# A two-layer cross-attention kernel: shared image values in layer 1, contexts laid out in pairs, and a fixed order for the first loads

## The chip, the cores and the metric

The kernel runs on one core of a Trainium2 chip. The metric is the device time of one execution in microseconds, lower is better. The engines are TensorE (PE, matrix products), VectorE (DVE), ScalarE (ACT), GpSimd (POOL) and SyncE (SP, which here issues nearly all DMAs).

## The reference

Two attention layers follow each other on x (16 images, 256 queries, 320 channels = 20 heads of 16). The context of an image has 256 tokens of 512 numbers. In layer 1, 77 are text tokens and 179 image tokens; in layer 2, 252 are text and 4 image. With s = 1/4:

```python
q = x @ Wq; k_text = text @ Wk; v_text = text @ Wv; ip_k = ip @ Wk_ip; ip_v = ip @ Wv_ip
text_out = softmax(q_h @ k_h.T * s) @ v_h                      # by head
scores = q_h @ ip_k_h.T * s
text_probs = softmax(q @ k_text.T * s)                         # all 320 channels, without heads
sem = (text_probs @ text) @ ip.T * s                           # 256 x 179
ip_out = (softmax(scores + 0.5 * sem) * spatial_mask) @ ip_v_h
x = (text_out + ip_out) @ Wout + bout + x
```

The second layer has the same form, with sem from the text probabilities of each head and normalized vectors.

## The kernel before

Each image of layer 1 is worked off in five slots of four heads; slot k = 5 b + g belongs to image b and heads 4g to 4g+3. Images 2c and 2c+1 form pair c. A matrix operand is split into a high and a low half (fp32r), and `prod` (L320) makes a product as three matmuls for each of the four 128-row tiles of the contexts: 12 matmuls.

In a slot PE computes S (L874: queries by keys, 128 queries in each of two halves), of which DVE takes the maxima of text and image columns. The maxima are transposed (L881), cast into `mt` and sent by DMA into a row of `qs`, the stack of queries; `ks` is the stack of keys, read from DRAM (`kd`), where the keys were stored with text first and image behind. Both stacks have 77 more rows for the semantic scores, which come from M (text tokens by image tokens, `tokens0`, the products of 77x192) and the text probabilities (`semantic0`, the matmuls X<-kb,q of L792). Then PE computes T, the scores with keys on partitions, less the maxima (L896); ACT exponentiates (L899) four pieces of 128x512, POOL multiplies each by `rs` (L902), and PE takes the products as moving operand with the values `vr` as weights (L934, `values0`, called from `attend0`), 24 matmuls a slot. The attend of slot k-1 stands in slot k.

The values of an image (`values0_`) are three products of 128 context tokens by 320 channels: tokens 0 to 127 by the text weights `wC`, tokens 0 to 127 by the image weights `wD`, tokens 128 to 255 by `wD`. Masks zero the rows that aren't text or image. In `values0` the value tile 0 is used by the first 16 of the 24 matmuls (text from tile 0, image from tile 0), and tile 1 by the last 8.

When each step of a task stands in the order is set by a table of slot times, STEPS: the name of a task (`k0` keys of a pair, `q0e`/`q0o` queries of the even and the odd image, `v0e`/`v0o` values, `m0e`/`m0o` tokens, `s0e`/`s0o` semantic, `c0` closing of an image; a 1 for layer 2, `w..` weights) and the slots, counted from the image's or pair's first, at which its steps are written. PE runs in exactly the order written; on the other engines a scheduler may reorder until `begun`. The steps ahead of the first slot are written one after the other in `begin`, and the first contexts and weights are loaded by `all_halves`, which issues the load of a tile and, when its ring is full, the casts of an older one. Loads of later contexts go through `context` and `in_turn`, with POOL making the low halves of a pair's second two tiles into `ctb` and its first two into `cta`.

## Time and profile before

| | |
|---|---|
| three runs | 1450.29, 1452.26, 1454.2 us |
| profiled execution | 1451.59 us, span 1449.8 us, granted clock 0.994 |
| PE, DVE, POOL, ACT busy | 97, 81, 79, 65% of the span |
| DMA | 215.74 MB, mean 149 GB/s |
| first T matmuls (L896) | 54.96 us |
| last value matmuls of layer 1's steady part, first of layer 2 | the stage 510.9 to 664.8 us |

A row of a timeline has the start in us from the span's begin, the duration of what was found in one piece, the engine, the line, the operation and the tiles (out<-in), the shapes and the count; in brackets the idle time ahead of it and what ended it. SPq rows are the times in which SP's queue issues DMAs; the data lands later. PEld is the load of PE's weights, which overlaps the products.

### The profile page before, as it was taken

What the parts mean: (1) busy time and instruction counts of PE and PEld (TensorE: products, weight loads), DVE (VectorE), ACT (ScalarE), POOL (GpSimd) and SP (SyncE); (2) the same over time, 40 slices, a digit from 0 to 9 for tenths busy, and PEclk for the clock granted to TensorE, in tenths of its full rate; (3) what the DMA queues carried; (4) which work ended last, traced back from release to release, by engine and by line L of the source; (5) the groups of instructions that cost most, each with busy time, mean ns of one, the idle gap of its engine ahead of it and who ended that gap; (6) DMA issues with size and microseconds to landing.
All of it is one profiled execution on the core that took longest, in us unless ns stands there. A gap on an engine that the chain in (4) does not pass through costs nothing.

```text
span 1449.8 us, 35042 instructions
## 1 busy us (share of the span) xinstructions
PE 1401.7 (97%) x12166; PEld 1157.8 (80%) x12166; DVE 1174.2 (81%) x2570; ACT 937.6 (65%) x2075; POOL 1152.3 (79%) x1181
## 2 busy tenths in 40 slices
PE   7899999999999999889999999999999999999998
PEld 6788888888888888577777788878878888888865
DVE  5477777777777788867888888988998889888887
ACT  5567676767676776755666666666666666566553
POOL 4269797979787878887778887788778877887785
PEclk9999999999999999999999999999999999999999
DMA  6866575665656578575544444544454445444411
GB/s 200 197 161 181 143 186 147 163 169 155 168 151 171 145 201 232 133 188 155 158 123 124 143 141 125 154 137 140 130 150 138 139 135 149 139 136 131 130 33 50
DMA packets 236284, 215.74 MB, mean 149 GB/s; under 512 B 57834, under 2 KB 222732, under 8 KB 236108
## 3 DMA queue, kind: packets, MB, share of 16 engines
q1 hardware_dynamic: 233886, 212.53, 53.4%
q8 instruction: 97, 1.59, 0.5%
q10 hardware_dynamic: 2222, 0.98, 0.3%
q14 instruction: 79, 0.65, 0.2%
HBM read 127.32 MB, written 85.16 MB: 147 GB/s over the span
## 4 chain that ended last, share of the span: by engine, by line
PE 52%; DVE 3%; POOL 1%; issue 1%; ACT 0%; DMA 0%; ACTq 0%; DVEq 0%; POOLq 0%
PE X L1075 18%; PE X L325 9%; PE X L725 6%; PE P L1088 5%; PE T L1018 4%; PE S L1023 3%; PE P L1090 2%; PE X L1209 1%; PE X L651 1%; PE P L1055 1%; DVE mn L1024 1%; PE P L934 1%; POOL P L902 0%; DVE wt L1078 0%; POOL wt L1066 0%
## 5 line engine op out<-in xcount | busy, mean ns | idle before, releaser
L902 POOL TENSOR_TENSOR P<-P,rs 128x512 f32<-128x512 f32 x320 | 412.4, 1313 | 136.1 <-ACT P L899 136.0
L1075 PE MATMUL X<-ctb,gm 128*128 128x512 f32 x1120 | 293.3, 403 | 0.7 <-DVE wt L1078 0.7
L1066 POOL TENSOR_TENSOR wt<-P,ctb 128x512 f32<-128x512 f32 x212 | 268.1, 1293 | 0.0
L899 ACT ACTIVATE P<-T 128x512 f32<-128x512 f32 x320 | 174.7, 594 | 101.8 <-PE T L896 83.7
L1024 DVE TENSOR_REDUCE mn<-S 128x4 fp32r<-128x1008 f32 x160 | 192.1, 1200 | 58.7 <-PE S L1023 56.8
L1075 PEld LDWEIGHTS X<-ctb,gm 128*128 128x128 f32 x1120 | 202.5, 190 | 38.5 <-DVE wt L1078 0.9
L1078 DVE TENSOR_TENSOR wt<-X,wt 128x512 f32<-128x512 f32 x240 | 159.7, 682 | 4.2 <-PE X L1075 3.9
L1030 ACT ACTIVATE P<-T 128x512 f32<-128x512 f32 x212 | 115.2, 598 | 58.3 <-PE T L1018 56.6
L1080 POOL TENSOR_TENSOR wt<-wt 128x512 f32<-128x512 f32 x80 | 103.5, 1294 | 60.2 <-DVE wt L1078 60.0
L876 DVE TENSOR_REDUCE mn<-S 128x4 fp32r<-128x716 f32 x160 | 142.5, 890 | 0.0
L1065 ACT ACTIVATE ctb<-P 128x512 fp32r<-128x512 f32 x212 | 122.4, 625 | 29.4 <-PE X L1075 20.6
L934 PE MATMUL P<-P,vr 128*32 128x256 f32 x1920 | 123.7, 388 | 0.0
L725 PE MATMUL X<-ho,wF 128*128 128x256 f32 x768 | 109.0, 286 | 2.2 <-DVE ho L974 1.2
L725 PEld LDWEIGHTS X<-ho,wF 128*128 128x128 f32 x768 | 100.5, 189 | 8.8 <-DVE ho L974 2.7
L725 PE MATMUL X<-hq,wE 128*128 128x256 f32 x720 | 102.7, 286 | 4.6 <-ACT hq L706 3.3
L725 PEld LDWEIGHTS X<-hq,wE 128*128 128x128 f32 x720 | 96.4, 193 | 8.3 <-ACT hq L706 3.8
L875 DVE TENSOR_REDUCE mn<-S 128x4 fp32r<-128x308 f32 x160 | 74.8, 468 | 23.2 <-PE S L874 22.9
L945 DVE STREAM_TRANSPOSE nt<-P 128x512 f32<-128x512 f32 x80 | 57.1, 714 | 39.2 <-PE P L934 38.9
L934 PEld LDWEIGHTS P<-P,vr 128*32 128x32 f32 x1920 | 56.1, 110 | 40.8 <-issue 4.9
L874 PE MATMUL S<-ks,qs 125*128 125x256 f32 x480 | 85.7, 301 | 2.2 <-DMA ks<-kd 1.7
L874 PEld LDWEIGHTS S<-ks,qs 125*128 125x128 f32 x480 | 64.4, 189 | 28.2 <-issue 24.1
L325 PE MATMUL X<-cta,wA 128*128 128x252 f32 (+3 forms) x534 | 78.8, 292 | 7.9 <-ACT wA L244 5.7
(231 smaller groups left out, 3275.3 us busy)
## 6 DMA issues: line engine op xcount, KB each, us to landing
qd<-q SPq DMA_DIRECT2D x80, 256.0 KB
qs<-qd SPq DMA_DIRECT2D x160, 112.0 KB
ks<-kd SPq DMA_DIRECT2D x160, 112.0 KB
rawc<-in_cT_dram SPq DMA_DIRECT2D x60, 256.0 KB
kd<-kst SPq DMA_DIRECT2D x50, 256.0 KB
qs<-qd SPq DMA_DIRECT2D x60, 192.0 KB
ks<-kd SPq DMA_DIRECT2D x60, 192.0 KB
qd<-q SPq DMA_DIRECT2D x64, 128.0 KB
```

What stands on the lines that cost most here:

```text
L325: last = mm(out, lhs(a, k), rhs(b, k), start=i == 0, stop=i == len(terms) - 1)
L725: mm(pp, w(s, k, slice(m * 128, (m + 1) * 128)), a[:, t], start=i == 0, stop=i == len(terms) - 1)
L874: mm(sp[:, h], Q[: XROW + T0, h, t * 128 : (t + 1) * 128], K[: XROW + T0, h], start=True, stop=True)
L876: anchor(nc.vector.tensor_reduce(mn[:, 1, :, t], sp[:, :, T0:], axis=AX.X, op=ALU.max))
L899: exp = anchor(nc.scalar.activation(pt, st[p], AF.Exp, scale=SCALE))
L902: anchor(nc.gpsimd.tensor_mul(pt, pt, rs[:, t : t + 1].to_broadcast([128, 2, S])))
L934: mm(pv[32 * s : 32 * s + 32, o : o + S], v[:, vt, h : h + 32], P[k, s // 2][:, t, s % 2], start=vt < 2, stop=vt != 1,)
L1024: anchor(nc.vector.tensor_reduce(maxes[k + 2][:, :, t], sp[:, :, :T1], axis=AX.X, op=ALU.max))
L1065: nc.scalar.activation(R[k, u][:, t], P[k, u][:, t], AF.Copy, scale=0.5)
L1066: anchor(nc.gpsimd.tensor_sub(W[k, u][:, t], P[k, u][:, t], f(R[k, u][:, t])))
L1075: mm(yp, gm[:, gb], R[k, u][:, kt], start=i == 0, stop=i == len(blocks[n]) - 1)
L1078: nc.vector.tensor_mul(product, yp, w[:, n])
```

## The change

- The contexts of a pair of layer 1 lie in one tile of 538 columns: 77 text of the even image, 179 image of the odd image, a gap of 26 zero columns, 179 image of the even image, 77 text of the odd. Each tile is loaded in three pieces (`bring`) instead of one.
- `values0_` makes two products for an even image and three for an odd one: the tile that holds image columns of both is multiplied once and evacuated twice, with masks, into the values of both images. For an even image the tile with the shared rows is 0; for an odd image it is 1, and `values0` uses it in the first 16 of the 24 matmuls. `attend0` sees to it that the shared product has been made.
- Text keys multiply 2 x 78 instead of 2 x 96 columns, the semantic scores of an image 154 instead of 192, tokens 180 instead of 192. The keys of an image lie in `kd` with text first for one of the pair and image first for the other, and the two indicator rows (which tell text from image columns) are in `kd` too: a load of the K stack brings 50 rows instead of 48.
- M is copied with all 256 columns into `ks`, before 179.
- In `project` the products with low halves of the right side come after those of the high ones.
- The first contexts and weights are loaded and cast in an order that is written out (BEGIN): of the contexts the text columns first, x of image 0 and the query weights next, image columns after them. Text keys are made tile by tile of the contexts.
- The output of the last image is sent in three pieces, each when it is done.
- Many entries of STEPS are other numbers.

```diff
+NI = S - T0
+GAP = 2 * T0 - 128
+PW = 2 * S + GAP
+TX, IM = (slice(NI, S), slice(0, T0)), (slice(0, NI), slice(T0, S))
+CT, CI = (PW - T0, 0), (T0, S + GAP)
+MIXED = (1, 0)
...
-    "k0": (-14.4, -13.3, -13, -12.4, -12, -10.8, -10.4, -9.8, -9.4, -8.8, -8.4,),
+    "k0": (-14.4, -13.3, -13, -12.4, -12, -10.8, -10, -9.4, -9, -8.4, -8,),
...
+BEGIN = """
+W2 C0 W0 C1 W1 C2 C3 W3 X0 Q0 Q1 Q2 c0 w0 T0 c1 w1 T1 c2 w2 T2 c3 w3 T3 I0 I1 q0:0 q0 q1 I2 I3 K0 K1 K2 q0:0
+i3 K3 e0 q2 V0 i0 i1 n0 q0:0 e1 e2 V1 V2 q0:0 i2 q0:0 q0:1 k0 k1 m0t:0 l1 q0:0 k2 l0 k3 l2 l3 V3 U0 U1 U2 U3
...
+    def bring(raw, src):
+
+        if src.shape[-1] == 2 * S:
+            for to, at, n in (0, 0, T0), (T0, S + T0, NI), (S + GAP, T0, S):
+                dma(raw[..., to : to + n], src[..., at : at + n])
+        else:
+            dma(raw, src)
...
     def values0_(b):
-        ct, i = ct0[b // 2], b % 2
-        V = vr[(b + 2) % 3]
-        for t, (w,), lo, sc in ((0, wv0, 0, tmask[:, 0:1]), (1, wvi0, 0, tmask[:, 1:2]), (2, wvi0, 128, 1.0)):
+        j, ring = 1 - b % 2, lambda b: vr[(b + 2) % 3]
+        V = ring(b)
+        parts = [(0, wv0, (PW - 128, 0)[j], 1), (2, wvi0, (CI[0], CI[1] + NI - 128)[j], 0)]
+        nc.vector.tensor_copy(vcols(V, V0W)[:, 0:2, :, 16], vmasks[j].unsqueeze(2).to_broadcast([128, 2, H]))
+        if b % 2:
+            parts.insert(0, (1, wvi0, S + T0 - 128, 1))
+        for t, (w,), lo, masked in parts:
             vp = bank()[:, :320]
-            prod(vp, lambda s, k: ct(s, k)[:, i, lo : lo + 128], lambda s, k: w(s, k), 4)
-            nc.scalar.activation(
-                vcols(V, V0W)[:, t, :, 0:16], vp.rearrange("p (h d) -> p h d", d=D), AF.Copy, scale=sc
-            )
+            prod(vp, lambda s, k: ct0[b // 2][k][:, s, lo : lo + 128], lambda s, k: w(s, k), 4)
+            for i in (j,) if t != 1 else (1, 0):
+                scale = vmasks[i][:, t : t + 1] if masked else 1.0
+                nc.scalar.activation(
+                    vcols(ring(b - i if t == 1 else b), V0W)[:, t, :, 0:16], vp.rearrange("p (h d) -> p h d", d=D), AF.Copy, scale=scale
+                )
+            if t == 1:
+                results["mixed", b // 2] = True
             yield
...
-        terms = [(s, k, t) for k in range(2) for s, t in ((0, k), (0, 3 + k), (1, k))] + [(0, 2, 2), (1, 2, 2)]
+        terms = [(s, k, k) for k in range(2) for s in range(2)] + [(0, 0, 3), (0, 1, 4), (0, 2, 2), (1, 2, 2)]
...
-                dma(K[T0 : T0 + XROW], stack_rows(kd[0][b // 2][:, :, b % 2])[:, hs])
+                dma(K[T0 : T0 + XROW + 2], kd[0][b // 2][:, 1 - b % 2].rearrange("(q h) t -> q h t", h=H)[:, hs])
...
-                    m = f(get("m0t", b)[:, 0:1, T0:]).to_broadcast([T0, 4, S - T0])
-                    order(nc.scalar.copy(K[:T0, :, T0:], m), *casts[-1:])
+                    m = f(get("m0t", b)[:, 0:1]).to_broadcast([T0, 4, S])
+                    order(nc.scalar.copy(K[:T0], m), *casts[-1:])
...
+        while ("mixed", b // 2) not in results:
+            step(("v0", b + 1))
...
     def values0(k, pv, v, vt):
-        t, o = ((0, 0), (0, S), (1, S))[vt]
+        mixed = MIXED[1 - k // NG % 2]
+        t, o = ((mixed, 0), (mixed, S), (1 - mixed, S))[vt]
...
+            if l * B + b == 2 * B - 1:
+                late(lambda: dma(out_d[b, m * 128 : (m + 1) * 128], y[:, m]))
```

The first place at which the order matters is SP's queue around the DMA that brings the first maxima into the stack (qs<-mt). The tiles kst and ho hold keys on their way to DRAM, rawc and raw receive contexts of the second pair. Before:

```order
L139 DMA rawc_92<-in_cT_dram 128x512
L139 DMA rawc_93<-in_cT_dram 128x512
L139 DMA raw<-in_cT_dram 128x512 x2
L139 DMA kd_66<-kst_237 128x2x256
L139 DMA kd_66<-kst_237 128x256
L139 DMA kd_66<-kst_238 128x2x256
L139 DMA kd_66<-kst_238 128x256
L139 DMA kd_66<-ho_239 64x77 x2
L139 DMA kd_66<-ho_239 64x179 x2
L139 DMA kd_66<-ho_239 64x77
L139 DMA kd_66<-ho_239 64x179
L884 DMA qs_188<-mt_198 2x8x128
```

Now:

```order
L155 DMA rawc_97<-in_cT_dram 128x256
L155 DMA raw<-in_cT_dram 128x77
L155 DMA raw<-in_cT_dram 128x179
L155 DMA raw<-in_cT_dram 128x256
L155 DMA raw<-in_cT_dram 128x77
L155 DMA raw<-in_cT_dram 128x179
L155 DMA raw<-in_cT_dram 128x256
L155 DMA kd_66<-ho_106 64x2x77
L155 DMA kd_66<-ho_106 64x2x179
L155 DMA kd_66<-ho_106 64x77
L155 DMA kd_66<-ho_106 64x179
L1007 DMA qs_117<-mt_630 2x8x128
L155 DMA kd_66<-kst_105 128x2x256
L155 DMA kd_66<-kst_105 128x256
```

The key stores from kst moved behind qs<-mt, the stores from ho are four rather than six rows, and contexts come as three pieces of a tile.

The second place is SP's first loads, after the change (before, contexts and key weights took turns and xq came behind them):

```order
L155 DMA P_94<-in_wk_dram 128x384
L155 DMA P_92<-in_cT_dram 128x2x77
L155 DMA P_92<-in_wk_dram 128x384
L155 DMA P_93<-in_cT_dram 128x2x77
L155 DMA P_93<-in_wk_dram 128x384
L155 DMA P_94<-in_cT_dram 128x2x77
L155 DMA P_95<-in_cT_dram 128x2x77
L155 DMA P_95<-in_wk_dram 128x384
L155 DMA xq_100<-in_xT_dram 128x3x256
L155 DMA P_92<-in_wq_dram 128x384
L155 DMA P_93<-in_wq_dram 128x384
L155 DMA P_94<-in_wq_dram 128x384
```

P takes the key weights and text columns (128x2x77); xq and the query weights stand directly behind.

The third place is PE in the last slot of an odd image's turn (slot 39), from its first T matmuls on. P_9x are the products that POOL makes (two tiles a slot), vr the values, wA the key weights: the matmuls of cta and ctb with wA are one product of text keys of the next pair. Before:

```order
L896 MATMUL T<-qs_188,ks_192 128x256 x4
L325 MATMUL X<-cta_82,wA_86 128x192 x3
L325 MATMUL X<-cta_83,wA_86 128x192 x3
L325 MATMUL X<-ctb_84,wA_86 128x192 x3
L325 MATMUL X<-ctb_85,wA_86 128x192 x3
L934 MATMUL P<-P_97,vr 32x256 x2
L934 MATMUL P<-P_98,vr 32x256 x2
L934 MATMUL P<-P_97,vr 32x256 x2
L934 MATMUL P<-P_98,vr 32x256 x2
L934 MATMUL P<-P_97,vr 32x256 x2
L934 MATMUL P<-P_98,vr 32x256 x2
L874 MATMUL S<-ks_194,qs_190 128x256 x4
```

Now:

```order
L1019 MATMUL T<-qs_117,ks_121 128x256 x4
L1060 MATMUL P<-P_94,vr 32x256 x2
L1060 MATMUL P<-P_95,vr 32x256 x2
L1060 MATMUL P<-P_94,vr 32x256 x2
L1060 MATMUL P<-P_95,vr 32x256 x2
L1060 MATMUL P<-P_94,vr 32x256 x2
L1060 MATMUL P<-P_95,vr 32x256 x2
L996 MATMUL S<-ks_123,qs_119 128x256 x4
L1019 MATMUL T<-qs_117,ks_121 128x256 x4
L933 MATMUL X<-ident,sp_387 77x128
L933 MATMUL X<-ident,sp_388 77x128
L356 MATMUL X<-cta_82,wA_86 128x156 x3
```

Before, the product of text keys stood between T and the attend; now the attend follows T directly, and the text keys come after it.

402 lines of the change are left out of this document (208 added, 194 removed), and 34 rows, old and new, of the table STEPS.

## The prediction

> **What bounds the kernel now.** I read the page's busy times first, then one table of stages, and then, stage by stage, the timeline of the engine that ends last there. First the totals and the stages; each cell is the busy time with the number of instructions.
>
> ```profile
> PE 1401.7 (97%) x12166; PEld 1157.8 (80%) x12166; DVE 1174.2 (81%) x2570; ACT 937.6 (65%) x2075; POOL 1152.3 (79%) x1181
> ...
> core 0: us, PE busy (x) PEld busy (x) DVE busy (x) ACT busy (x) POOL busy (x), PEclk, DMA share, GB/s
> 0.00:55.00 55.00, 39.77 (x244) 37.05 (x244) 25.93 (x68) 29.91 (x67) 17.80 (x37) 0.97 0.71 202
> 55.00:102.20 47.20, 43.16 (x356) 37.23 (x357) 34.50 (x74) 29.70 (x69) 27.46 (x23) 0.96 0.70 182
> 102.20:510.90 408.70, 408.55 (x3844) 354.07 (x3843) 302.43 (x728) 298.02 (x656) 350.35 (x312) 1.00 0.62 161
> 510.90:664.80 153.90, 140.53 (x1327) 115.86 (x1325) 123.48 (x276) 101.24 (x226) 127.01 (x122) 0.99 0.71 184
> 664.80:1449.80 785.00, 769.68 (x6404) 613.65 (x6403) 687.91 (x1425) 478.69 (x1060) 629.67 (x691) 1.00 0.45 130
> ```
>
> TensorE (PE) is busy 97% of the span. From 102.2 to 510.9, the steady part of layer 1, it is busy 408.55 of 408.70 us: a pair of images there costs what its matmuls cost, and other engines count only where they make PE wait. The stage before the first T matmuls (0 to 55) is different: PE works 39.77 of 55 us, so 15.2 are lost. The next stage loses 4.0, the change of layers (510.9 to 664.8) 13.4, and layer 2 15.3 of 785. The sum is made against the profiled execution's own time, 1451.59 us, which lies 0.67 below the median of the runs, 1452.26.
>
> **The start.** These are rows of the loads, PE and the DMA queue of SP, on the way to the first T matmuls.
>
> ```profile
> 0.00:5.00 5.00, 0.00 (x0) 0.00 (x0) 0.28 (x3) 2.06 (x3) 4.43 (x11) 1.00 0.59 168
> 5.00:18.00 13.00, 9.70 (x37) 8.06 (x37) 11.12 (x32) 9.41 (x23) 11.26 (x22) 1.00 0.84 276
> ...
> 12.41 0.42 SPq L139 DMA_DIRECT2D xq<-in_xT_dram  x1
> ...
> 17.81 0.38 PE L725 MATMUL X<-hq,wE 128*128 128x256 f32 x1 [1.83 <-ACT hq L706]
> 18.54 4.52 PE L725 MATMUL X<-hq,wE 128*128 128x256 f32 x23 [0.34 <-DVE hq L707]
> ...
> 30.22 1.12 PE L325 MATMUL X<-ctb,wA 128*128 128x360 f32 x6
> ...
> 33.20 3.65 SPq L139 DMA_DIRECT2D kd<-ho  x6
> ...
> 38.36 0.33 SPq L139 DMA_DIRECT2D ks<-kd  x1
> ...
> 44.16 0.71 PE L874 MATMUL S<-ks,qs 125*128 125x256 f32 x4 [1.67 <-DMA ks<-kd]
> ...
> 45.24 3.67 SPq L139 DMA_DIRECT2D kd<-kst  x4
> ...
> 49.01 3.74 SPq L139 DMA_DIRECT2D kd<-ho  x6
> 49.35 0.24 ACT L883 CAST mt<-X 16x128 fp32r<-16x128 f32 x1
> ...
> 52.86 0.70 SPq L884 DMA_DIRECT2D qs<-mt  x1
> ...
> 54.96 0.71 PE L896 MATMUL T<-qs,ks 127*128 127x256 f32 x4 [3.13 <-DMA qs<-mt]
> ```
>
> Before, the input of the queries (xq) was issued only at 12.41, behind all contexts and key weights. So the first query matmul stood at 17.81 and the queries ended at 23.06. Everything afterwards hangs in one chain: image keys (the last at 30.22 to 31.34), their stores (six small ones from ho, 3.65 us of SP), the load of ks at 38.36, S at 44.16, the maxima, and their DMA qs<-mt. That DMA is the clearest loss: its source mt was cast by 49.59, and it was issued at 52.86, since SP was held by four key stores (3.67) and six more (3.74), which belong to the second image.
>
> After the change the order of SP is: four key weights with four narrow text columns, then xq, three query weights, then the image columns, then the image-key weights. Bytes ahead of the query weights' end are 4 x 197 KB (key weights), 4 x 79 (text), 393 (xq) and 3 x 197: about 2.08 MB, 7.5 us at the 276 GB/s of the row, plus some 2 us of start (the first 5 us moved 168 x 5 = 0.84 MB, which takes 3.0 at that rate). The image columns end at 2.81 MB, 12.2 us. But the cast of the third query weight stands on ACT behind that of the last image column, so it ends around 14, and the queries near 18.6 to 19: about 4 us sooner. The image keys then end near 27.4 and not 31.34, and with four stores from ho in place of six (2.4 instead of 3.65 us) ks loads near 34, S follows near 40.2. Six new loads of two indicator rows into kd cost SP about 2.6 us, but they stand ahead of the stores while those still wait for their casts. After S, only four ho stores (2.4) and twelve context pieces (12 x 0.45 from the 0.91 for two) stand ahead of qs<-mt, and the kst stores have moved behind it: issue near 44.6, first T near 47, so **-8 us**. PE's work ahead of the first T is one product of 12 value matmuls smaller (below); all else of the 8 is idle time. Bounds: if only the kst stores' 3.67 us move out of the way and the rest is given back, -3.3; if no queue holds the chain up, S by 37 and T by 44, -11. I take -8 since each step has its own row. Key stores moved behind qs<-mt are late next: text of the second image is then read from kd later, in slots that begin some 30 us after.
>
> **Values of layer 1.** The contexts of a pair now lie in one buffer (text even, image odd, a gap of 26 columns, image even, text odd), and the 128-column tile that straddles both is multiplied once: five value products a pair instead of six.
>
> ```profile
> 308.11 0.70 PE L325 MATMUL X<-cta 128*77 128x192 f32 x6
> ...
> 309.17 1.07 PE L325 MATMUL X<-wC,cta 128*128 128x320 f32 x6
> ...
> 310.95 0.22 PE L881 MATMUL X<-ident_r,mn 128*16 128x128 f32 x1
> ...
> 352.42 1.48 PE L792 MATMUL X<-kb,q 128*128 128x192 f32 x12
> 353.74 0.22 PE L881 MATMUL X<-ident_r,mn 128*16 128x128 f32 x1
> ```
>
> A product is 12 matmuls of 320 columns. From the first row to the transpose behind it is 310.95 - 309.17 = 1.78 us, 148 ns each. So 8 x 1.78 = 14.2 us of PE work go: one in the start (inside the -8), one in pair 1, six in the steady part. ACT evacuates the shared tile twice, so its instructions stay as many.
>
> The same buffer narrows other matmuls: text keys from 192 to 156 columns, semantic scores from 192 to 154, tokens from 192 to 180. The semantic product's 12 take 353.74 - 352.42 = 1.32 us, 110 ns each, with 128 weight columns. Tokens' 12, also of 192 columns but with 77 weight columns, take 309.17 - 308.11 = 1.06 us, 88 ns. The moving side is equal, and the time differs by the weights: so 110 ns is the weights' loading, and narrowing the moving side brings nothing there, only about 0.1 us a pair in the tokens. I take 0; the other end is the slope between 110 ns at 192 columns and 148 at 320, 0.30 ns a column, or 384 matmuls x 37 x 0.30 = 4.2 us. The Trainium skill, page "TensorE: Matmul & The Clock Gate", section "LDWEIGHTS (loading the stationary operand)", has the load last by the number of weight columns, P/1.2 ns (107 for 128, 64 for 77). The trace's 110 agrees, its 88 lies above 64; by that rule too the narrowing brings nothing. The same page's section "Back-to-back issue gap" gives N/2.4 + 2.5 ns for a single matmul; by that alone the estimate would be -5.8 us, and the 110 ns at 192 columns (82 by the formula) speak against it here.
>
> **Who waits once PE is faster.** An odd image's attend (24 matmuls on the products of exponentials by rs) now uses tile 1 in its first two passes, where before only the last 8 of the 24 did. POOL makes tile 1's products last. So PE must wait for POOL's end at the attend's begin.
>
> ```profile
> 325.53 2.54 POOL L902 TENSOR_TENSOR P<-P,rs 128x512 f32<-128x512 f32 x2 [0.39 <-ACT P L899]
> 330.43 2.80 POOL L902 TENSOR_TENSOR P<-P,rs 128x512 f32<-128x512 f32 x2 [2.37 <-ACT P L899]
> ...
> 341.89 1.31 SPq L139 DMA_DIRECT2D rawc<-in_cT_dram  x2
> ...
> 346.87 1.14 ACT L244 CAST ctb<-rawc 128x512 fp32r<-128x512 f32 x2
> ...
> 346.58 2.56 POOL L902 TENSOR_TENSOR P<-P,rs 128x512 f32<-128x512 f32 x2 [0.82 <-ACT P L899]
> 349.10 2.51 POOL L245 TENSOR_TENSOR ctb<-rawc,ctb 128x512 fp32r<-128x512 f32 x2
> ...
> 352.00 5.20 POOL L902 TENSOR_TENSOR P<-P,rs 128x512 f32<-128x512 f32 x4
> ...
> 358.83 5.04 POOL L902 TENSOR_TENSOR P<-P,rs 128x512 f32<-128x512 f32 x4
> ...
> 356.21 1.67 PE L934 MATMUL P<-P,vr 128*32 128x256 f32 x24
> ...
> 362.84 0.81 PE L325 MATMUL X<-cta,wA 128*128 128x192 f32 x6
> ...
> 364.25 1.50 PE L934 MATMUL P<-P,vr 128*32 128x256 f32 x24
> ```
>
> In the slot of 356.21 the attend began 0.99 us before POOL's four products ended (352.00 + 5.20 = 357.20), which was possible only since tile 1 came last. Now PE comes 1.8 us sooner and cannot start before POOL is done. POOL is not at its limit: ahead of these products it idled 2.37 and 0.82 us for exponentials. If PE runs ahead, these come sooner, and POOL takes back about 3.2, less 0.26 (four context subtractions of 538 rather than 512 columns) less about 1.3 for the slot whose T moves behind the shared product. Its end comes near 355.5, PE near 354.4: a wait of 1.1. In the next slot PE also loses a cover: a text-key product (362.84 to 364.25) moves behind the attend; POOL's end (358.83 + 5.04, some 1.7 sooner) is near 362.2 and PE there near 362.06: 0.15. So of 1.78 + 0.1 saved per pair, 1.1 are lost and 0.8 kept: **-5 us** in six pairs. Bounds: nothing kept, 0; all kept, -11.3. Pair 1, whose stage has idle time already, **-1** (0 to -1.9).
>
> Contexts are loaded in three pieces a tile rather than one, so two tiles hold SP for 6 x 0.45 = 2.7 us instead of 1.31 (row 341.89). The cast came 3.7 us after the second issue (346.87), most of it the loads' flight, and the subtraction at 349.10 after it; 0, with the price of the other end under D. Copies of M into K grow by 43% (77x1024 for 77x716), on ACT, and casts of keys into kst come in two pieces, 16 more each on ACT and DVE; these are busy 298 and 302 of 408.7 us in the steady part: 0, as long as exponentials come ahead of POOL. Loads of ks carry 50 rows for 48: 0, as SP's count of them stays.
>
> **The end and smaller things.**
>
> ```profile
> 1442.51 3.14 PE L725 MATMUL X<-ho,wF 128*128 128x256 f32 x23 [0.40 <-DVE ho L972]
> ...
> 1445.69 0.48 DVE L996 SCALAR_TENSOR_TENSOR xq<-X,bo,xq 128x256 f32<-128x256 f32 x1 [0.47 <-PE X L725]
> 1446.20 0.38 SPq L139 DMA_DIRECT2D out_dram<-xq  x1
> ```
>
> The last image's output leaves as one DMA at 1446.20; the span ends 3.6 us later. Now each third is sent when its columns are done, so the last piece is 131 KB and not 393. A third of the flight is not to be had, since part of the 3.6 is fixed: **-1.1** (bounds 0 and -2.4). In the output projection the products of low halves stand third at the earliest rather than second, which takes PE's 0.40 us of waiting for ho off, in the last image: **-0.4**; elsewhere PE does other work. The change of layers and the first layer-2 images have new slot times in the order table; nothing in the trace prices them, and the 13.4 us idle could shrink or grow: 0, bounds -4 and +4.
>
> **Sum.** -8 - 1 - 5 - 1.1 - 0.4 = -15.5: 1451.59 becomes 1436.1, by the median about 1437.
>
> **Rivals.** B, PE alone: POOL keeps up and the seven pairs keep 1.88 each, -13.2 for -6; the sum is -22.7, by the median 1430. For it: PE's 100% and POOL's 3.2 us idle a pair; against it: the 0.99 us by which the attend already leads POOL. N, narrower matmuls are cheaper by the slope, -4.2 more: 1433; against it 110 against 88 ns at one width. C, the start is given back: T comes early, but the stage to 102.2 has DMA busy 0.70 and PE idle 4.0, and layer 1's pairs wait for POOL as far as the bounds allow. Then the start brings -3.3, the pairs 0, the end -1.1: 1448; with the change of layers at +4, 1452. D, slower: a context piece that lands late blocks POOL, because its subtraction stands in order ahead of the products of that slot. Each us of it goes straight to PE, six pairs over. It decides from (15.5 + 4.4)/6 = 3.3 us late a pair; a late 4 us gives 1460. For it the 1.4 us of longer issue and pieces of 308 bytes; against it the 2.23 us between the cast's begin and the subtraction. E, the value products do not become fewer: excluded, since the written order holds 96 fewer.
>
> **How the numbers follow.** Forecast .48 (range of its own 1431 to 1442, start and pairs by half their bounds); B .18; N .05; C .23, of which half is within 0.3%; D .06. A measurement tells about 0.3%, 4.4 us, from no change. Faster: .48 + .18 + .05 + .13 = .84; same .10; slower .06. The range reaches to B with all bounds low (1423) and to C's middle (1449).
>
> **What the changed profile would show.** Right: first T near 47 and qs<-mt issued near 45; 192 rather than 288 value products on wD, each still 147 to 148 ns; the semantic 12 still 1.3 us; a wait of about 1 us on POOL ahead of the attends of an odd image's fourth slot; a steady pair near 73.4 us instead of 74.2; the last output DMA a third as long. Wrong: first T later than 51 (the chain at the start sits elsewhere), a pair below 72.6 (B) or not below 74.2 (C, D), or more than 17 us idle at the change of layers.

## The result and the profile after

The changed kernel takes 1461.8 us (1461.47 to 1462.72), the kernel before 1453.08 in the same comparison: a ratio of 1.0064, 95% interval 1.0045 to 1.0082, slower by 0.64%. The forecast was 1437. The profiled execution's span went from 1449.8 to 1460.1 us.

These are the totals and the first four of the same stages as before.

```profile
PE 1397.2 (96%) x12070; PEld 1151.6 (79%) x12070; DVE 1190.7 (82%) x2618; ACT 951.6 (65%) x2106; POOL 1150.9 (79%) x1189
...
0.00:55.00 55.00, 38.92 (x231) 37.27 (x231) 27.25 (x83) 31.45 (x78) 16.92 (x45) 0.90 0.69 186
55.00:102.20 47.20, 41.30 (x323) 36.39 (x325) 29.56 (x65) 26.22 (x61) 20.96 (x18) 0.89 0.73 199
102.20:510.90 408.70, 397.98 (x3725) 340.99 (x3715) 318.75 (x743) 300.36 (x659) 346.62 (x308) 1.00 0.61 158
510.90:664.80 153.90, 139.39 (x1317) 116.04 (x1317) 124.58 (x287) 107.92 (x237) 127.97 (x122) 0.99 0.72 186
```

PE works 4.5 us less in sum (1397.2 for 1401.7), and in the stage from 102.2 to 510.9 it is now idle for 10.7 us, where it had been idle for 0.15. The shared values alone were to take 14.2 us off PE's work. The clock granted to PE fell from 0.97 and 0.96 to 0.90 and 0.89 in the first two stages. The starts of each image's first T matmuls, read from the timeline, tell where the time went:

| image's first T at, us | 0 | 1 | 2 | 4 | 12 | layer 2 | its last image | end of span |
|---|---|---|---|---|---|---|---|---|
| before | 54.96 | 102.2 | 139.2 | 213.9 | 510.9 | 664.8 | 1383.8 | 1449.8 |
| after | 56.46 | 106.4 | 143.9 | 219.5 | 521.5 | 673.9 | 1395.6 | 1460.1 |
| later by | 1.5 | 4.2 | 4.7 | 5.6 | 10.6 | 9.1 | 11.8 | 10.3 |

The start loses 4.2 us, each steady pair 1.2 (75.5 for 74.2, of which odd images 39.5 for 38.5), layer 2 about 0.2 an image (48.35 for 48.15); the change of layers (152.4 for 153.9) and the end gain 1.5 each. The 510.9 and 664.8 us that bound the stages are the first T matmuls of image 12 and of layer 2.

SP's queue at the start, after:

```profile
24.66 4.12 SPq L155 DMA_DIRECT2D kd<-kst  x4
28.84 4.71 SPq L155 DMA_DIRECT2D kd<-in_ind_dram  x6
33.59 2.69 SPq L155 DMA_DIRECT2D kd<-ho  x4
...
38.12 0.31 SPq L155 DMA_DIRECT2D ks<-kd  x1
...
40.06 7.98 SPq L155 DMA_DIRECT2D rawc<-in_cT_dram  x6
48.27 3.28 SPq L155 DMA_DIRECT2D raw<-in_cT_dram  x6
51.59 2.58 SPq L155 DMA_DIRECT2D kd<-ho  x4
54.27 0.76 SPq L1007 DMA_DIRECT2D qs<-mt  x1
```

PE there:

```profile
16.50 3.49 PE L846 MATMUL X<-hq,wE 128*128 128x256 f32 x17 [1.72 <-DVE wE L473]
...
27.68 1.16 PE L356 MATMUL X<-ctb,wA 128*128 128x360 f32 x6
31.57 2.07 PE L846 MATMUL X<-hq,wE 128*128 128x256 f32 x8 [2.73 <-ACT hq L827]
...
45.22 1.19 PE L996 MATMUL S<-ks,qs 125*128 125x256 f32 x8 [1.82 <-DMA ks<-kd]
...
56.46 1.20 PE L1019 MATMUL T<-qs,ks 127*128 127x256 f32 x4 [4.79 <-DMA qs<-mt]
```

The steady pair: PE from an odd image's value product on; then DVE and POOL around the same image's first slot.

```profile
338.45 1.12 PE L356 MATMUL X<-wC,cta 128*128 128x320 f32 x6 [1.40 <-DVE tmp L1077]
...
359.50 1.47 PE L914 MATMUL X<-kb,q 128*128 128x154 f32 x12
360.80 0.22 PE L1004 MATMUL X<-ident_r,mn 128*16 128x128 f32 x1
...
364.47 1.49 PE L1060 MATMUL P<-P,vr 128*32 128x256 f32 x20 [0.57 <-POOL P L1025]
```

```profile
332.68 1.35 DVE L618 COPY vr<-vmask 128x40 f32<-128x40 f32 x1 [0.22 <-PE P L1060]
...
335.25 0.88 DVE L999 TENSOR_REDUCE mn<-S 128x4 fp32r<-128x716 f32 x1
...
336.41 1.56 DVE L830 SCALAR_TENSOR_TENSOR hq<-hq,tmask,xq 128x256 fp32r<-128x256 f32 x1
337.90 0.41 DVE L1077 TENSOR_TENSOR tmp<-nt,P 128x256 f32<-128x256 f32 x1
...
332.67 5.02 POOL L1025 TENSOR_TENSOR P<-P,rs 128x512 f32<-128x512 f32 x4 [0.41 <-ACT P L1022]
337.65 1.46 POOL L828 TENSOR_TENSOR hq<-xq,hq 128x512 fp32r<-128x512 f32 x1
```

Two things stand in these rows. PE waits 1.40 us for a bank of results that DVE hands back late, and 0.57 on POOL at the fourth slot. And DVE is late since two of its instructions are long: the copy of mask columns into vr, 128x40, takes 1.35 us, and the last step of the queries' split, 128x256, 1.56. In the first three images, where POOL is idle, the copy takes 0.17 to 0.20; in the odd images before, the split's step took 0.49:

```profile
331.59 0.49 DVE L709 SCALAR_TENSOR_TENSOR hq<-hq,tmask,xq 128x256 fp32r<-128x256 f32 x1 [0.19 <-ACT hq L706]
```

Here the copy ends at 334.03, about when the first of POOL's four products ends (332.67 + 5.02 / 4 = 333.93), and the step at 337.97, 0.28 us after the fourth (337.69). Before, POOL was busy beside the step too (the row 330.43 of the prediction, two products), but the running product had only 0.13 us left when the step began. So the step's length is set by how much of POOL's running instruction is left, not by POOL being busy as such. A reduction from PSUM (335.25, 0.88) beside the same POOL products has its usual length.

### The profile page after: what moved, and what is told of

Read it like the earlier page. It is cut to its first block, busy times and chain, and to the rows that moved or that the text cites. A ratio compares the mean times of both kernels' runs of the same rounds, so it can differ in the third digit from the quotient of the medians.

```text
span 1460.1 us, 35029 instructions
## 1 busy us (share of the span) xinstructions
PE 1397.2 (96%) x12070; PEld 1151.6 (79%) x12070; DVE 1190.7 (82%) x2618; ACT 951.6 (65%) x2106; POOL 1150.9 (79%) x1189
## 4 chain that ended last, share of the span: by engine, by line
PE 80%; DVE 6%; POOL 4%; DMA 3%; ACT 3%; issue 3%; SPq 1%; ACTq 0%; DVEq 0%; POOLq 0%
PE X L1203 17%; PE X L356 17%; PE X L846 11%; PE P L1060 7%; PE S L996 5%; PE P L1216 5%; PE T L1146 4%; PE T L1019 4%; PE S L1151 3%; POOL P L1025 2%; PE P L1218 2%; SPq L155 1%; PE X L1337 1%; DMA ks<-kd 1%; PE X L772 1%
## 5 line engine op out<-in xcount | busy, mean ns | idle before, releaser
L1158 ACT ACTIVATE P<-T 128x512 f32<-128x512 f32 x212 | 115.4, 598 | 53.9 <-PE T L1146 52.3
L1060 PE MATMUL P<-P,vr 128*32 128x256 f32 x1920 | 127.5, 383 | 4.6 <-POOL P L1025 4.1
L998 DVE TENSOR_REDUCE mn<-S 128x4 fp32r<-128x308 f32 x160 | 74.8, 468 | 20.6 <-PE S L996 20.5
L356 PE MATMUL X<-wC,cta 128*128 128x320 f32 x480 | 81.1, 315 | 5.6 <-DVE tmp L1077 5.6
L1019 PE MATMUL T<-qs,ks 127*128 127x256 f32 x480 | 79.1, 288 | 6.6 <-DMA qs<-mt 5.0
```

Of the source, the lines that this page charges most:

```text
L356: last = mm(out, lhs(a, k), rhs(b, k), start=i == 0, stop=i == len(terms) - 1)
L1019: mm(st[p][:, j], K[:KS0, 2 * p + j, t * 128 : (t + 1) * 128], Q[:KS0, 2 * p + j], start=True, stop=True)
L1060: mm(pv[32 * s : 32 * s + 32, o : o + S], v[:, vt, h : h + 32], P[k, s // 2][:, t, s % 2], start=vt < 2, stop=vt != 1,)
```

## The experiments

Ratios are to the kernel before, run on the same chip. Where a profiled execution met the stall that the runs c_best and f_hq are about, each such image was some 6 to 7 us longer. Executions without a profile that lie as far above their kernel's shortest (three of e_act's ten, at 1461 to 1462) may have met it too; that isn't shown. Medians of such kernels lie above their shortest runs.

| run | what | median us | ratio, 95% interval |
|---|---|---|---|
| the change | | 1461.8 | 1.0064 (1.0045 to 1.0082) |
| e_act | mask columns copied by ACT | 1455.04 | 1.0022 (1.0004 to 1.0040) |
| e_order | odd images' tile order | 1461.8 | 1.0055 (1.0034 to 1.0077) |
| e_queue | qs<-mt ahead of contexts | 1467.78 | 1.0101 (1.0073 to 1.0128) |
| e_marks | indicator rows early | 1460.87 | 1.0054 (1.0039 to 1.0069) |
| p_copy | before, plus the copy | 1456.26 | 1.0025 (1.0013 to 1.0037) |
| l_proj | e_act, old order in project | 1457.59 | 1.0027 (1.0011 to 1.0043) |
| l_steps | e_act, old t1 and o1 | 1458.16 | 1.0035 (1.0019 to 1.0051) |
| e_one | e_act, 4 loads for 12 | 1452.8 | 0.9992 (0.9977 to 1.0007) |
| e_both | e_act and e_order | 1452.78 | 1.0002 (0.9989 to 1.0015) |
| e_casts | e_one, start rearranged | 1452.56 | 0.9994 (0.9978 to 1.0011) |
| e_six | e_act, product made twice | 1474.74 | 1.0150 (1.0133 to 1.0167) |
| c_best | e_casts, e_both, old t1 and o1 | 1450.96 | 0.9989 (0.9972 to 1.0006) |
| f_hq | c_best, split's step off DVE | 1448.22 | 0.9968 (0.9957 to 0.9980) |
| f_proj | f_hq, old order in project | 1447.04 | 0.9961 (0.9949 to 0.9973) |
| f_tab | f_hq, old table at the change of layers | 1454.77 | 1.0007 (0.9997 to 1.0016) |

### The copy (e_act, p_copy)

```diff
-        nc.vector.tensor_copy(vcols(V, V0W)[:, 0:2, :, 16], vmasks[j].unsqueeze(2).to_broadcast([128, 2, H]))
+        nc.scalar.copy(vcols(V, V0W)[:, 0:2, :, 16], vmasks[j].unsqueeze(2).to_broadcast([128, 2, H]))
```

> The changed kernel with one edit: the copy of the mask columns into vr, one a layer-1 image, is made by ACT and not by DVE. In the changed kernel's profile it takes DVE 0.17 to 0.20 us while POOL has nothing to do and 1.2 to 1.35 us in the steady part. Theory P (this copy waits for POOL's instruction, and DVE's delay keeps a bank of results from the next value product): the wait of the product X<-wC of 1.4 us a pair falls below 0.4, a steady pair from 75.5 to 74.0-74.4 us, the whole by 7 to 9 us to 1453-1455. Rival R (PE comes to the banks earlier because its own work shrank; the copy is short enough to be hidden): the wait stays above 1.0 us, the pair within 0.3 of 75.5, the whole within 2 us of 1461.8.

PE's waits in the steady stage by line and releaser (sum in us, times, longest), the changed kernel first, then e_act:

```profile
PE X L356 <- DVE tmp L1077: 5.6, 4, 1.4
PE P L1060 <- POOL P L1025: 2.9, 5, 0.6
```

```profile
PE P L1060 <- POOL P L1025: 2.9, 5, 0.6
PE S L996 <- DVE mn L999: 2.6, 5, 0.8
```

The bank's wait is gone, the split's step beside the copy is back from 1.56 us to 0.59, a pair takes 74.0 us for 75.5 (odd images 38.3 for 39.5, even 35.7 for 36.0), and the whole falls by 6.8 us in the medians, just short of the 7 to 9 expected, from 1.0064 to 1.0022. Theory P holds; R falls.

The other way about, p_copy adds the copy to the kernel before (line 504 there).

```diff
         V = vr[(b + 2) % 3]
+        nc.vector.tensor_copy(vcols(V, V0W)[:, 0:2, :, 16], tmask[:, 0:2].unsqueeze(2).to_broadcast([128, 2, H]))
```

> The kernel before with one addition: at the start of each image's values a DVE copy of the mask columns into vr (128x40, the same values that are there already), as the changed kernel makes it. It measures the disputed cost by itself. Theory P (such a copy waits for POOL's instruction): it takes 0.2 us at the start and 1.2 to 1.35 in the steady part; since DVE is the slower part of the chain from attend to the next results' bank, a steady pair goes from 74.2 to 74.6-75.5 and the whole by 2 to 8 us. Rival R (only the changed order of work makes the copy matter): the copy is long, but the pair stays within 0.2 of 74.2 and the whole within 1.5 us.

DVE's copy in two images, and POOL beside each:

```profile
328.92 0.21 DVE L504 COPY vr<-tmask 128x40 f32<-128x40 f32 x1
...
365.94 1.46 DVE L504 COPY vr<-tmask 128x40 f32<-128x40 f32 x1 [1.02 <-PE P L935]
...
326.08 2.54 POOL L903 TENSOR_TENSOR P<-P,rs 128x512 f32<-128x512 f32 x2 [0.40 <-ACT P L900]
330.98 1.29 POOL L903 TENSOR_TENSOR P<-P,rs 128x512 f32<-128x512 f32 x1 [2.36 <-ACT P L900]
...
364.81 2.53 POOL L903 TENSOR_TENSOR P<-P,rs 128x512 f32<-128x512 f32 x2
```

One instruction, two lengths. At 328.92 POOL is between 328.62 and 330.98 without work, and the copy takes 0.21. At 365.94 POOL is in two products that end at 367.34, and the copy ends at 367.40. Of 16 copies 3 met POOL so, and two steady images with such a copy took 36.2 us for 35.7. The whole rose by 2.5 us, of which these two images show 1.0; where the rest went isn't shown. So the mechanism is P's, and its price a matter of where the copy stands; that all images would pay was wrong.

The Trainium skill, page "SBUF — State Buffer", section "Who interferes with whom", says that DVE and GpSimd share a pair of ports as an exclusive lock, which a DVE copy in its two-port mode takes; that a DVE instruction with two inputs in SBUF contends with a GpSimd instruction that reads SBUF; and that tensor_reduce never contends on trn2. The rows agree: 1.35 and 1.46 for 0.2, 1.56 for 0.49, 0.88 for the reduction.

### The attend's order (e_order, e_both) and the product (e_six)

```diff
-        for vt in range(3):
+        for vt in (range(3) if b % 2 == 0 else (2, 1, 0)):
             values0(k, pv, v, vt)
...
-                start=vt < 2,
-                stop=vt != 1,
+                start=vt == 0 or vt == (1, 2)[k // NG % 2],
+                stop=vt == 0 or vt == (2, 1)[k // NG % 2],
```

> The changed kernel with one edit: in odd images the attend uses the pure image tile (0) in its first 8 matmuls and the mixed tile (1) in the last 16; before the edit 16 of tile 1 came first. Theory O (POOL makes the products of tile 1 last and PE waits for them, 1.2 us a pair): the waits on POOL fall to at most 0.4 us a pair, the pair by 0.8 to 1.2 us, the whole by 5.5 to 8 us to 1454-1456. Rival: PE then meets the bank that DVE gives back late (the 1.4 us) later or with more wait, and the whole falls by less than 3 us.

```profile
PE X L356 <- DVE tmp L1077: 5.6, 4, 1.4
...
PE P L1060 <- POOL P L1025: 0.9, 5, 0.2
```

The waits on POOL fell from 2.9 to 0.9 in five, as expected, and the 1.4 us for DVE stayed. A pair took 74.8 us for 75.5, a little less than expected; but the whole lay only 0 to 1.3 us lower. In this profile the start was later (image 2 at 146.3 for 143.9) and the change of layers longer (154.9 for 152.4), which takes back what the pairs gained; the edit gives no reason for the later start. The rival's number held, its reason not: the 1.4 us didn't grow.

> The kernel e_act (mask columns copied by ACT) with the attend's order of odd images as in e_order (pure image tile first). In e_act a steady pair takes 74.0 us, with PE waiting 0.58 on POOL at the fourth slot and 0.5 on DVE's maxima. Theory O (with the copy gone, the products of tile 1 are what PE waits for): the wait on POOL falls below 0.25, the pair to 73.2-73.5 us, the whole by 3 to 6 us against e_act (1455.0), to 1449-1452. Rival D (POOL and DVE are themselves near the pair's length, so PE's wait only moves): the pair stays at 73.8 to 74.1, the whole within 1.5 us of 1455.

With the copy gone as well, the pair took 73.6 (35.7 and 37.85), between the two theories and close to the 73.4 that the prediction had; the whole went from 1.0022 to 1.0002.

e_six makes the shared product twice:

```diff
-            prod(vp, lambda s, k: ct0[b // 2][k][:, s, lo : lo + 128], lambda s, k: w(s, k), 4)
+            for again in range(2 if t == 1 else 1):
+                prod(vp, lambda s, k: ct0[b // 2][k][:, s, lo : lo + 128], lambda s, k: w(s, k), 4)
```

> The kernel e_act with the shared value product made twice, one after the other into the same bank (12 more matmuls of 320 columns a pair, 96 in all; the second overwrites the first). It asks what the product that the change saves is worth on the path: 1.76 us of PE a pair. If PE sets the pair, 74.0 becomes 75.5 to 75.8 and the whole rises by 12 to 14 us; if waits on POOL and DVE set it, part of it fills them: the pair becomes 74.4 to 75.0, the whole rises by 4 to 8 us.

A steady pair took 75.9 us (35.7 and 40.2) for 74.0, so the product's 1.76 us come out in full. The whole rose by 19.7, more than the 12 to 14 expected: in this profile one steady odd image took 45.9 for another reason (below), and image 2 began 3.6 us later and the change of layers took 157.8 us for e_act's 152.1; these last two are not explained. In the steady part a product more costs on the path what its matmuls take.

### The start (e_marks, e_queue, e_one, e_casts)

e_marks moves `m0` in BEGIN from behind `stack:0:M` to behind `V2`.

> The changed kernel with one edit at the start: the six loads of the indicator rows into kd are issued at about 15 us, ahead of the query stores, not between the key stores of kst and ho (28.8 to 33.6). Theory S2 (they stand on the path to the first S): the ho stores start near 29.9 rather than 33.6, S at 41.5-42.5 rather than 45.2, T 2.5 to 3.5 us earlier, and the whole falls by 2.5 to 4 us to 1458-1459. Rival (the way through the semantic scores, which feeds the stacks too, is as long): S is less than 1 us earlier and the whole within 1 us of 1461.8.

T came at 53.9, image 1 at 104.2 and image 2 at 141.9, 2 us sooner, and layer 2 at 674.0 for 673.9: the 2 us were lost again at the change of layers. The whole fell by about 1 us. The stores of ho began at 31.4 and S at 43.9, half as much sooner as expected. S2 held for T, not for the end.

e_queue moves `max:0` ahead of `k0:1` (the contexts) and `O2`.

> The changed kernel with one edit at the start: the first maxima's DMA qs<-mt is issued ahead of the twelve context pieces and the four text stores of ho, not behind them. Theory S1 (SP's queue holds it, each DMA waiting for the landing of the one eight earlier): it is issued near 50 us in place of 54.3, the first T matmuls at 51.5-52.5 in place of 56.5, and the whole falls by 3.5 to 5 us to 1457-1458. Rival (the contexts of pair 1 then come late and the keys of pair 1 wait): T is early, but the image that starts at 143.9 starts less than 1 us earlier, and the whole is within 1.5 us of 1461.8.

Up to image 1, PE waited in this kernel:

```profile
PE T L1019 <- ACT P L1022: 7.6, 2, 5.1
...
PE T L1019 <- DMA qs<-mt: 0.5, 1, 0.5
```

```profile
54.51 0.64 ACT L268 CAST cta<-rawc 128x538 fp32r<-128x538 f32 x1 [1.73 <-DMA rawc<-in_cT_dram]
...
56.42 1.08 ACT L1022 ACTIVATE P<-T 128x512 f32<-128x512 f32 x2
```

T came at 50.4, 6.1 us sooner, and image 1 at 108.0, 1.6 later. PE's wait moved from qs<-mt to the exponentials: ACT works in its order, and casts of the second pair's contexts, which had not landed, stood ahead of them. S1's cause was right and its gain wrong; the whole became slower than either theory said. The profile is of the shortest of the four executions (1464.2 us); what makes the others 1 to 9 us longer is not shown.

> The kernel e_act with the contexts of pair 1 loaded by one DMA a tile (four in all) in place of three (twelve), the columns being put in their places by the casts (8 more on ACT and on DVE). Theory S1' (SP's queue is held at the start since each DMA waits until the one eight earlier has landed): qs<-mt is issued at 49 to 50.5 and not 54, without later contexts; T at 51.5 to 53, image 1 at 102 to 103.5 and not 105.6; the whole falls by 2 to 4 us against e_act, to 1451-1453. Rival (as with qs<-mt ahead of the contexts: casts on ACT stand in the way): T is early, image 1 is not, and the whole stays within 1 us of 1455.

```profile
41.17 0.99 SPq L155 DMA_DIRECT2D rawc<-in_cT_dram  x2
43.23 3.54 SPq L155 DMA_DIRECT2D raw<-in_cT_dram  x2
47.26 5.66 SPq L155 DMA_DIRECT2D kd<-ho  x4
53.03 0.76 SPq L1015 DMA_DIRECT2D qs<-mt  x1
```

Four loads rather than twelve brought qs<-mt to 53.03 only. The stores behind them took the time instead (5.66 us for four). What SP's queue waited for from 38 to 56 us tells why, in the changed kernel and then in e_one:

```profile
SPq L155 <- DMA ks<-kd: 4.7, 3, 2.4
```

```profile
SPq L155 <- DMA ks<-kd: 6.0, 3, 2.9
```

In the trace each of SP's DMAs waits on the semaphore of the DMA eight issues earlier, so for its landing. In the changed kernel the three loads of ks stand eight issues before the fourth, sixth and eighth piece of the contexts, in e_one before the fourth load and two of the stores of ho: whatever DMA has that place inherits the wait. The number of pieces, which I had blamed, was a small part: from the last ks load to qs<-mt it was 12.3 us for 14.6. Why the loads of ks land as late as they do isn't shown. T came at 55.2 and image 1 at 105.3, as in e_act; the gain of 2 us in the median lies within the spread of both.

> The kernel e_one (mask columns by ACT, contexts of pair 1 in four DMAs) with three moves at the start: indicator rows early as in e_marks, qs<-mt ahead of the contexts as in e_queue, and the casts of those contexts behind the first exponentials on ACT. In e_queue T came at 50.4 and was given back, since the exponentials stood on ACT behind casts that waited for the contexts. Theory S3 (that order of ACT was what gave it back): T at 47 to 49, image 1 at 98 to 101 in place of 105.3, the whole by 3 to 6 us to 1447-1450. Rival (contexts and keys of the pair come too late in any case): T early, image 1 no earlier than 104, the image after it late, the whole within 2 us of 1452.8 or above.

T at 48.7 and image 1 at 102.6, for 55.2 and 105.3: of 6.5 us 2.7 survived. The three moves were made together, so what each is worth is not separated. S3 was right about T, missed its 98 to 101 for image 1, and puts the start level with the kernel before (102.2), no better. Its executions spread from 1448.3 to 1460.2.

### What spreads the executions (c_best, f_hq)

> All of it: e_casts, the attend's order of e_both, and the entries t1 and o1 of the order table as before. If the parts add up, the whole is 1443 to 1448, faster than before by 0.4 to 0.7%; if the pair is held by POOL and DVE and the start by the contexts, it is 1450 to 1454, the same as before.

Its shortest execution took 1447.95 us, its longest 1459.66, the median 1450.96, in the range of the second case, and the ratio is not told apart from 1. In the profiles of e_both, e_casts and e_six one or two odd images took 44 to 46 us, for 38 (40 in e_six). Such an image in e_casts, DVE first, then POOL and PE:

```profile
205.34 7.28 DVE L838 SCALAR_TENSOR_TENSOR hq<-hq,tmask,xq 128x256 fp32r<-128x256 f32 x1
...
203.21 5.04 POOL L1033 TENSOR_TENSOR P<-P,rs 128x512 f32<-128x512 f32 x4
208.17 1.32 POOL L836 TENSOR_TENSOR hq<-xq,hq 128x512 fp32r<-128x512 f32 x1
209.41 0.49 POOL L1090 TENSOR_TENSOR hsn<-tmp 128x128 f32<-128x128 f32 x1
209.82 2.52 POOL L1033 TENSOR_TENSOR P<-P,rs 128x512 f32<-128x512 f32 x2
216.59 1.27 POOL L1033 TENSOR_TENSOR P<-P,rs 128x512 f32<-128x512 f32 x1 [4.25 <-ACT P L1030]
...
214.16 1.22 PE L1004 MATMUL S<-ks,qs 125*128 125x256 f32 x4 [4.37 <-DVE mn L1007]
```

The split's last step, 0.48 us long when POOL is idle (at 33.66 of this profile), took 7.28 us on DVE: POOL ran eight instructions from 203.21 to 212.34 without a gap, six of them begun after DVE's (the products take some 1.25 us each), and DVE came through only when POOL ran out of work. PE then waited 4.37 us for the maxima behind it, and the granted clock was 0.50 from 213 to 219 us; the image is 6.2 us longer than the next odd one, more than the wait. The Trainium skill, page "SBUF — State Buffer", section "Who interferes with whom", has the pair of ports held "for the whole instruction" by whoever issues first, where it speaks of DVE's two-port mode; here the one that waited lost it again to instructions begun later, up to the end of the row.

In most images the step gets in at the next end of a POOL instruction. In the same profile, the same place of the next odd image:

```profile
285.99 0.71 DVE L838 SCALAR_TENSOR_TENSOR hq<-hq,tmask,xq 128x256 fp32r<-128x256 f32 x1
...
283.89 5.19 POOL L1033 TENSOR_TENSOR P<-P,rs 128x512 f32<-128x512 f32 x4
```

There, as at 205.34, the running product had 0.43 us left when the step began. What decides between the two, no run shows. The profiles of e_act, e_one and c_best, with the same step on DVE, have no such image; in l_proj and l_steps it took 4.2 us in image 1.

```diff
-            nc.vector.scalar_tensor_tensor(hl[:, 2], f(hl[:, 2]), neg, src[:, 2], op0=ALU.mult, op1=ALU.add)
+                order(nc.scalar.activation(hl[:, 2], f(hl[:, 2]), AF.Copy, scale=neg))
+                order(eng.tensor_add(hl[:, 2], f(hl[:, 2]), src[:, 2]))
```

> The kernel c_best with the last step of the split of the queries' input in layer 1 (hq<-hq,tmask,xq, 128x256, two inputs in SBUF) taken from DVE: ACT multiplies, POOL adds. In e_both, e_casts and e_six this step was found once or twice at 6.9 to 7.3 us on DVE, beside a row of POOL products without a gap, and the image was 6.6 us longer. Theory P2 (a DVE instruction with two SBUF inputs, too, waits for POOL, and for a whole row of its instructions if they follow without a gap): no such image is left, the executions lie within 3 us of each other, around 1447 to 1449. Rival (the 7 us are something else, or POOL's 0.7 us more an image cost as much): executions above 1455 stay, or all are 2 to 5 us longer than c_best's shortest, 1448.

Seven executions lie between 1447.4 and 1451.5, none long, and the ratio is 0.9968. The 4.1 us between them are more than the 3 expected, and seven executions without a long one say little where c_best had one in nine; f_proj's six and f_tab's ten, without the step on DVE as well, lie within 5.5 us each. P2 is borne out by the long step's rows more than by these times. POOL pays for the addition: an even image takes 36.4 for 35.7, an odd one 37.45 for 37.9.

### Layer 2 and the table (l_proj, l_steps, f_proj, f_tab)

> The kernel e_act (the changed one with the mask columns copied by ACT) with the old order of terms in project. An image of layer 2 takes 48.35 us in the changed kernel and 48.15 before. If the new order of terms is the cause, an image goes back to 48.15 and the whole falls by 2 to 3 us against e_act (to about 1452.5); if not, layer 2 stays at 48.3 to 48.4, and the whole stays at 1455 or rises by up to 1 us, since products of ho then wait for DVE.

> The kernel e_act with eight entries of the order table for layer 2 put back to those before (t1, o1, their entries for images 0 and 1, i1 of the last but one image, c1 of the last). If these entries are the cause of the 0.2 us more an image of layer 2, an image goes back to 48.15 and the whole falls by 2 to 4 us against e_act (to 1451-1453); if not, an image stays at 48.3 to 48.4 and the whole within 1 us of 1455.

An image of layer 2 took 48.35 us with the old order in project, as without, and 48.25 with the old t1 and o1: half of the 0.2. Neither showed in the whole, whose executions spread by 12 and 6 us.

> The kernel f_hq with the old order of terms in project. With t1 and o1 as before, an image of layer 2 takes 48.3 us in c_best against 48.15 before. If the order of terms is the rest, it is 48.15 here and the whole 1 to 2.5 us less than f_hq; if not, 48.25 to 48.35 and the whole within 1 us of f_hq or above.

> The kernel f_hq with the order table's entries for the change of layers as before (w7, w6, w2, w4, i1 of the last but one image, c1 of the last). In the changed kernel the stage from image 12 of layer 1 to the third image of layer 2 takes 250.1 us, before 250.9. If the new entries are worth something, this one is 1 to 4 us longer than f_hq; if they are neutral, it is within 1 us.

f_proj is 1.2 us below f_hq, within both intervals. Its image stays at 48.25, so that part of the expectation fell; only the second image of layer 2 went from 51.0 to 48.3 us. f_tab is 6.5 us longer: image 12 to layer 2 takes 161.2 us for 153.5. So in f_hq the new table entries are worth 6.5 us, more than the 1 to 4 guessed.

f_proj beats both kernels: 0.39% faster than before and, by the two ratios, about 1% faster than the change. Its steady stage:

```profile
102.20:510.90 408.70, 405.73 (x3794) 347.96 (x3798) 299.42 (x740) 313.62 (x701) 359.93 (x326) 1.00 0.65 161
```

PE is idle 3.0 us in the stage where the changed kernel had 10.7. Two of f_proj's parts, the split's step off DVE and the order of the first loads, have no need of shared values; the kernel before with these parts was not run.

## Why the prediction was wrong, point by point

The profiled span was to become 15.5 us shorter and became 10.3 longer, 25.8 apart. The start makes 12.2 of these (-8 forecast, +4.2 at image 1's first T), layer 1 from there to image 12 makes 12.4 (the pairs' -6, and +6.4), layer 2 2.7 (0, and +2.7 over fifteen images); the change of layers takes 1.5 off. Both signs of being wrong that the prediction named came: a first T later than 51 and a pair not below 74.2.

- **The start, -8.** Failed; +1.5 at the first T, +4.2 at image 1. The first half came as worked out: queries ended at 19.99 (16.50 + 3.49), forecast 18.6 to 19; image keys at 28.84, forecast 27.4. Then the six indicator loads took 4.71 us, not 2.6, and did not stand ahead of the waiting stores but between those of kst and ho, whose casts were done. So ks loaded at 38.12 and not 34. The second error is "twelve context pieces (12 x 0.45)": they took 11.3 us, since an issue waits for the landing of the DMA eight issues earlier, here the loads of ks. The row of the kernel before (3.67 us for four key stores) had such waits in it too; it was read as the price of these stores, so moving them was taken to save it. The third is that I let a sooner T stand for a sooner kernel: e_queue had its T at 50.4 and lost more behind it, and e_casts, whose T at 48.7 is near the 47 forecast, began image 1 at 102.6, no sooner than before. At lower granted clock (0.90 for 0.97) matmuls also took longer: the T group at 56.46 took 1.20 us, 0.71 before. The Trainium skill, page "TensorE: Matmul & The Clock Gate", section "What's actually happening", has the clock follow PE's recent activity; the trace agrees in that the granted clock was 0.50 from 31 to 37 and from 55 to 61 us, behind PE's gaps of 2.73 and 4.79 us. Before, a gap of 3.13 us ahead of T was followed by no such stretch (T took 0.71), so the gap's length alone does not tell. An estimate from the rows of the first two stages: 0.07 less granted clock over 55 and over 47.2 us is 7.2 us of full clock lost; in part of that time PE was idle, so the clock may be all of the 4.2 or little. No run separates it.
- **Shared values, 14.2 us of PE.** Right for the product: 12 matmuls fewer a pair, PE busy on wD for 5.87 us of a pair and not 7.73, and e_six shows 1.9 us a pair on the path. Not for PE as a whole: a steady pair keeps it busy for 73.45 us, before 74.24, so 0.8 less (1.3 in e_act), and of the difference the attend's 240 matmuls, at 15.71 us for 15.19, are about half. Why they take longer is not shown. The counts on wD are 288 for 384, not 192 for 288; the difference, 96, is right.
- **Narrower matmuls, 0.** Right: 12 of 154 columns took 360.80 - 359.50 = 1.30 us, of 192 columns 1.32. Rival N is out. (By the formula named there, 384 matmuls and 37 columns come to -5.9, not -5.8.)
- **Waits on POOL, 1.1 and 0.15 a pair.** The place was right, the size half of that as idle time: 0.57 in the fourth slot and none in the next, since PE came later than worked out. The sum took off only the 1.1; with the 0.15 it would have kept 0.63 a pair, 3.8 us in six and not 5.
- **DVE's additions at 0, because DVE is busy 302 of 408.7 us.** This step failed most. I listed the casts and never priced the mask columns' copy, and I argued from busy time. The copy lasts until POOL's running product ends, it stands ahead of the transposes and maxima that give banks back, and e_act shows 6.8 us for it. With it and the attend's order mended (e_both) a pair took 73.6 us, where 73.4 had been forecast. The profile before showed the means to see it: the split's step had 0.49 us in odd images of layer 1 and 1.2 in layer 2, at one shape.
- **The end, -1.1.** Right in sign: 64.5 us from the last image's T to the end, for 66.0. e_act took 62.95 with the same ending, so that the size fits is in part luck. **project, -0.4**: not seen (62.9 in f_proj with the old order, 62.9 in f_hq with the new). **The change of layers, 0 within 4**: 152.4 for 153.9, inside the bounds. **Layer 2** had no term of its own: +2.7, of which the entries t1 and o1 make about half.
- **The rivals.** Slower had .06, by late contexts that block POOL. It came by another way, which no rival had.

What stays open: some 0.1 us an image of layer 2, how the start's 4.2 us divide between transfers, ACT's order and the clock, and why a waiting DVE instruction gets in at one end of a POOL instruction and not at another.

## What to carry to other kernels

An instruction's length is not its own where two engines share a way to memory: before adding a small DVE copy, look for the same operation in the profile with two lengths, and at what the other engine does then; if in doubt, give it to an engine that does not share. At the start, follow the chain past the event that comes sooner: the next wait (here ACT's order) decides what is kept. On a DMA queue, the time of an issue's row may be a wait for an earlier DMA: see what it waits for before counting the row as that issue's price. When a change loses by one careless instruction, its gain may still be there: with that and one more instruction moved, the attend's order turned and the start rearranged, the kernel with shared values is 0.39% faster than before; how much of this the shared values are is not shown.

## What the runs showed of the hardware

- A DVE instruction with two inputs in SBUF waited for the rest of a row of eight POOL instructions (7.28 us for 0.48, e_casts), not for one; at the same place of the next odd image it took 0.71. In both it ended some 0.3 us after the end of a POOL instruction, as in the changed kernel (337.97 after 337.69).
- The same DVE copy took 0.21 or 1.46 us in one execution of one kernel, by whether POOL was idle.
- A DMA's issue on SP, 0.33 to 0.45 us when free, took 1.3 on average for six pieces of contexts (7.98 us): in this program an issue waits for the landing of the DMA eight issues earlier, and 4.7 us of the start's waits were for loads of ks.
- The granted clock was 0.50 for some 6 us behind waits of PE of 2.73, 4.79 (the changed kernel) and 4.37 us (e_casts), and stayed 1.00 behind one of 3.13 (the kernel before).
